# End of a recurrence on one core: where the last tile's squares are summed, and which PSUM banks the two halves use

## Chip, cores and metric

The kernel runs on 1 core of one Trainium2 chip. The metric is the device time of one execution, in microseconds (us). All data is fp32. Engines: PE (matmul; PEld is its weight load), DVE (VectorE), ACT (ScalarE), POOL (GpSimd), SP (issues DMAs).

## What is computed

The reference has two layers. The first is a recurrence over 1024 tokens for each of 4 x 1024 channels, run forward and backward, and a quotient of its two sums, gated by a sigmoid. The second works on its output x in two blocks: normalised logits of 16 slots against all tokens, the best 4 tokens per slot, a gather of those rows, and an attention of all tokens over the slots.

```
def step(carry, x):
    a, b = carry
    ekv_t, ek_t = x
    a = a * decay + ekv_t
    b = b * decay + ek_t
    return ((a, b), (a, b))
...
num = nf + nb - ekv + euk * vf
den = df + db - ek + euk
base = jax.nn.sigmoid(r.astype(jnp.float32)) * (num / jnp.maximum(den, 1e-08))
out = base * (0.8 + 0.2 * tf)
...
for _ in range(NB):
    logits = _rms(x, norm_pre_w) @ compete_w.T + compete_b
    slot_logits = jnp.swapaxes(logits, 1, 2)
    vals, idx = jax.lax.top_k(slot_logits, k_eff)
    ...
```

So a logit is the product of a token's row with a slot's weights, divided by the root of the mean of that row's squares. The change concerns how those two sums, products and squares, are finished at the end of the first layer.

## The kernel before

Channels lie on the 128 partitions and tokens along the free axis: a tile is 128 channels x 1024 tokens, and there are 32 tiles (4 batches b x 8 channel groups k), i = 8 b + k, run by the loop at L587. For each tile DVE runs the scans (L323, numerator's backward scan L411), ACT the exponentials and a guess of 1/denominator by Ln and Exp (L426, L428), POOL multiplications (L302, L308, L405, L441, L442, L465), and DVE a Newton step (L452). PE adds the scans into the numerator `num` in PSUM (L373, by the identity matrix), turns the finished tile for storing (L493) and contracts it. The finished tile overwrites its gate tile (`gate`), its squares overwrite `quo` (ACT, L468).

The order on each engine is the order of the code: `pin` keeps it. Waits are put in by a tracker of reads and writes of tiles.

`contract` (L470 to L483) multiplies a tile by the slots' weights (`lhs[:, k]`, source `gate`) or its squares by a column block of ones (`lhs[:, NK]`, source `quo`). Both give 32 rows of `raw`, at partitions 32 b: rows 0 to 15 hold the logits' sums, 16 to 31 the sums of squares. `raw` is one PSUM tile of two banks, 512 tokens in each. At the end the sums of squares lie on other rows than the logits they belong to, so for each half (h = 1 first, then 0) `spread_squares` (L723) copies `raw` to SBUF on DVE (L724) and multiplies it by the matrix `spread` (L725), which puts a square sum on each of the logits' rows, in the PSUM tile `sq`.

The end of the recurrence is L696 to L781, for the last tile, i = 31. In program order: guess in halves; for each half the numerator's backward scan (L416), POOL's products (L438), the addition on PE; contractions of tile 30 among these; then for each half Newton step, product on DVE (L465) and square on ACT (L468); then contractions of tile 31: gate and squares of half 1, gate of half 0; spread of half 1; squares of half 0. Then `norm_root` (ACT: Ln L738, Exp L740, Square L741) and `norm_logits` (DVE: L746, L748, L753, L757, a Newton step on 1/root, and the bias) for half 1, spread of half 0 between them, and the same for half 0. Last, 16 transposes of tiles 30 and 31 (L773) into four banks, four copies on ACT (L779), two stores of rows from ACT's queue (L510), and `hold_clock` (L112), which multiplies the identity by a constant into a bank that nobody reads, seven times.

What follows is the same code for both blocks (`write_slots`): maximum and index on DVE (L833 to L838), the token numbers put in columns by PE (`token_ps`, L851) and cast (L860), an indirect gather of rows on POOL (L863), which needs the stored rows in memory, `hold_clock` again (L885, five in the first block), and the multiplication of the gathered rows (`pmix`, L892), then `pw` (L910), `pkv` (L960), `pk` (L1030). From there on PE works through 32 groups of 128 tokens in each block.

PSUM's tags at the end: `own` (2 banks), `num` (2), `raw` (2), `ptr` (1), `columns` (1).

Of the kernel before, what the change touches and what calls it, by code (L numbers as in the profile page):

```python
# [10 lines left out]
F32 = mybir.dt.float32  # L11
U32 = mybir.dt.uint32
AF = mybir.ActivationFunctionType
ALU = mybir.AluOpType
# [4 lines left out]
P = 128  # L19
B, L, D = 4, 1024, 1024  # L20
S, K, NB = 16, 4, 2
H = 16
HD = D // H
NK = D // P
# [4 lines left out]
EPS = 1e-6  # L29
# [9 lines left out]
def kernel(  # L39
# [25 lines left out]
    nc = tc.nc  # L65
# [12 lines left out]
    pin = tc.keep_in_program_order  # L78
# [33 lines left out]
    def hold_clock(bank, n):  # L112

        for _ in range(n):
            pin(nc.tensor.matmul(bank, ident, npost_bc[:, :512], start=True, stop=True))
# [5 lines left out]
    rec_ps = rec_stack.enter_context(tc.tile_pool(name="rec_ps", bufs=1, space=PSUM))  # L121
# [77 lines left out]
    lhs = rc.tile([P, NK + 1, 2, S], F32, name="lhs")  # L199
# [37 lines left out]
    half = rc.tile([P, B], F32, name="half")  # L237
# [21 lines left out]
    with rec_stack:  # L259

        columns = rec_ps.tile([P, 512], F32, tag="columns", bufs=1, name="columns")
# [2 lines left out]
        nc.vector.tensor_copy(dec_ps, decay)  # L264


        raw = rec_ps.tile([P, L], F32, name="raw")


        HK = NK // 2  # L270
# [40 lines left out]
        def own_tile(i):  # L311
            return rec_ps.tile([P, L], F32, tag="own", bufs=1, name=f"own_{i}")
# [58 lines left out]
        def add(num_ps, h, src, by=ident):  # L371
            pin(
                nc.tensor.matmul(  # L373
                    num_ps[:, ts(h, 512)], by, src, start=False, stop=True, skip_group_check=True
                )
            )
# [44 lines left out]
        def guess(i, both, parts=(every,)):  # L421

            quo = rec.tile([P, L], F32, tag="quo", bufs=2, name=f"quo_{i}")
            b = i // NK
            for part in parts:
                pin(nc.scalar.activation(quo[:, part], both[:, 0, part], AF.Ln))  # L426
                pin(
                    nc.scalar.activation(  # L428
                        quo[:, part],
                        quo[:, part],  # L430
                        AF.Exp,
                        scale=-1.0,
                        bias=half_log_gain[:, b : b + 1],
                    )
                )
            return quo
# [7 lines left out]
        def newton(i, both, quo, num_ps, part=every, out=None):  # L444

            b = i // NK
            den = both[:, 0, part]
            num = num_ps[:, part]
            if out is None:
                den, num = parted(den, i), by_half(num)  # L450
            pin(
                nc.vector.scalar_tensor_tensor(  # L452
                    den if out is None else out[:, part],
                    den,
                    twice_root[:, b : b + 1],
                    num,
                    ALU.subtract,
                    ALU.mult,
                    reverse0=True,
                )  # L460
            )

        def product(i, factor, engine, part=every):
            xk = gate_of(i)[:, part]
            pin(engine.tensor_tensor(xk, xk, factor[:, part], ALU.mult))  # L465

        def square(i, quo, part=every):
            pin(nc.scalar.activation(quo[:, part], gate_of(i)[:, part], AF.Square))  # L468

        def contract(i, src, w, halves=(0, 1)):  # L470

            b, k = i // NK, i % NK
            rows_b = slice(32 * b, 32 * b + 32)
            for h in halves:
                pin(
                    nc.tensor.matmul(  # L476
                        raw[rows_b, ts(h, 512)],
                        lhs[:, w].rearrange("p h s -> p (h s)"),
                        src[:, ts(h, 512)],
                        start=(k == 0 and w == NK),  # L480
                        stop=(k == NK - 1 and w == (NK if i == N - 1 else k)),
                    )
                )  # L483

# [82 lines left out]
        N = B * NK  # L567
        ek, ekv, both, edge, own, quo, num_ps = {}, {}, {}, {}, {}, {}, {}
        flat, pairs, by = {}, {}, {}
        halves = [ts(0, 512), ts(1, 512)]  # L570
# [125 lines left out]
        i = N - 1  # L696
        halves = [(h, ts(h, 512)) for h in (1, 0)]
        raw_sb = rec.tile([P, L], F32, tag="ov", bufs=1, name="raw_sb")
        sq = rec_ps.tile([P, L], F32, tag="own", bufs=1, name="sq")
        eps_col = rc.tile([P, 1], F32, name="eps_col")  # L700
        nc.gpsimd.memset(eps_col, EPS)
        spread_cols = spread.rearrange("p b h s -> p (b h s)")
        quo[i] = guess(i, both[i], [part for _, part in halves])
        square(i - 1, quo[i - 1])

        def contract_half(j, squares, h):
            contract(j, quo[j] if squares else gate_of(j), NK if squares else j % NK, (h,))

        for n, (h, part) in enumerate(halves):
            numerator_half(i, both[i], edge[i], h)  # L710
            gated(i, both[i], quo[i], part)
            add(num_ps[i], h, both[i][:, 1, part])
            if n == 0:
                contract_half(i - 1, False, h)
        contract_half(i - 1, True, 1)
        for squares in (False, True):
            contract_half(i - 1, squares, 0)
        for h, part in halves:
            newton(i, both[i], quo[i], num_ps[i], part, num_ps[i])
            product(i, num_ps[i], nc.vector, part)  # L720
            square(i, quo[i], part)

        def spread_squares(h, part):  # L723
            pin(nc.vector.tensor_copy(raw_sb[:, part], raw[:, part]))  # L724
            pin(nc.tensor.matmul(sq[:, part], spread_cols, raw_sb[:, part], start=True, stop=True))  # L725

        for squares in (False, True):
            contract_half(i, squares, 1)
        contract_half(i, False, 0)
        spread_squares(*halves[0])  # L730
        contract_half(i, True, 0)
        store_turned(i)
        root = rec.tile([P, L], F32, tag="quo", bufs=2, name="root")
        square_root = rec.tile([P, L], F32, tag="ekv", bufs=2, name="square_root")

        def norm_root(part):
            pin(
                nc.scalar.activation(root[:, part], sq[:, part], AF.Ln, scale=1.0 / D, bias=eps_col)  # L738
            )
            pin(nc.scalar.activation(root[:, part], root[:, part], AF.Exp, scale=-0.5))  # L740
            pin(nc.scalar.activation(square_root[:, part], root[:, part], AF.Square))  # L741

        def norm_logits(part):

            t = square_root[:, part]
            pin(nc.vector.scalar_tensor_tensor(t, sq[:, part], EPS * D, t, ALU.add, ALU.mult))  # L746
            pin(
                nc.vector.scalar_tensor_tensor(  # L748
                    t, t, -3.0 * D, root[:, part], ALU.add, ALU.mult
                )  # L750
            )
            pin(
                nc.vector.scalar_tensor_tensor(  # L753
                    t, t, -0.5 / D, raw[:, part], ALU.mult, ALU.mult
                )
            )
            pin(nc.vector.tensor_scalar_add(logits[:, part], t, cb_col))  # L757

        norm_root(halves[0][1])
        spread_squares(*halves[1])  # L760
        norm_logits(halves[0][1])
        norm_root(halves[1][1])
        norm_logits(halves[1][1])

        banks = [rec_ps.tile([P, NT, P], F32, tag="num", bufs=1, name="turn")]
        banks = [
            rec_ps.tile([P, 4, P], F32, tag=tag, bufs=1, name=f"turn_{tag}")
            for tag in ("ptr", "columns")
        ] + [banks[0][:, :4, :], banks[0][:, 4:, :]]
        for n in range(4):  # L770
            for q in range(4):
                block = gate_of(i - 1 + n // 2)[:, ts(4 * (n % 2) + q, P)]
# [3 lines left out]
        for j, stage in ((i - 1, staged(i - 1)), (i, stage_last)):  # L776
            for h in range(2):
                bank = banks[2 * (j - i + 1) + h]
                pin(nc.scalar.copy(stage[:, 4 * h : 4 * h + 4, :], bank))  # L779
            send(j, stage)  # L780
        hold_clock(rec_ps.tile([P, 512], F32, tag="ptr", bufs=1, name="idle"), 7)  # L781
    rc_stack.close()
    keep = ctx.enter_context(tc.tile_pool(name="keep", bufs=1))

# [21 lines left out]
    def bank(tag, name, bufs=2):  # L806
        return wps.tile([P, 512], F32, tag=tag, bufs=bufs, name=name)
# [4 lines left out]
    def write_slots(blk, begin_loads, early, begin):  # L812
# [5 lines left out]
        first, last = blk == 0, blk == NB - 1  # L818
# [63 lines left out]
            pin(nc.gpsimd.memset(score_bias[:, :, C:], 0.0))  # L882
            pin(nc.gpsimd.memset(bias_rows, 0.0))
        early()
        hold_clock(bank("po", f"idle_rows{blk}"), 5 if first else 1)  # L885

        mix_t = half_row(f"mix_t{blk}")
        pmix = bank("psc", f"pmix{blk}")
        for j in range(2):
            for k in range(NK):  # L890
# [5 lines left out]
                        start=(j == 0 and k == 0),  # L896
                        stop=(j == 1 and k == NK - 1),
# [9 lines left out]
        for k in range(NK):  # L907
            for h in range(2):
# [5 lines left out]
                        start=(k == 0),  # L914
                        stop=(k == NK - 1),
# [6 lines left out]
        for h in range(2):  # L922
            part = slots[:, ts(h, 512)]
# [3 lines left out]
        for h in range(2):  # L927
            pt = turned(f"pslots{blk}_{h}").rearrange("p q c -> p (q c)")[:, : 4 * R]
            part = slice(4 * h, 4 * h + 4)
# [92 lines left out]
        for g in range(2):  # L1022
            for i in range(NK):
# [3 lines left out]
                for q in range(4):  # L1027
# [6 lines left out]
                            start=True,  # L1034
                            stop=True,
# [10 lines left out]
            for q in range(4):  # L1046
# [6 lines left out]
                        start=True,  # L1053
# [387 lines left out]
```

## Time and profile before

| | us |
|---|---|
| runs | 1081.12, 1081.73, 1086.94; median 1081.73 |
| the profiled execution | 1085.4 |
| its span, first to last instruction | 1083.2 |
| PE busy | 991.9 (92%) |
| DVE / ACT / POOL busy | 739.6 / 516.1 / 548.1 |
| share of the chain that ended last | PE 59%, POOL 19%, ACT 9%, issue 7%, DVE 3%, DMA 2% |
| last scan's end in the recurrence, to pmix | 394.11 to 426.16 |

The profile is one execution. Every start below is counted from the span's start. The chain of work that ended last is followed back from the last instruction: each step is released by the one before it, or stands behind it on its engine. "Issue" in it is time in which nothing shown was waited for. A PE row counts passes: an fp32 multiplication is two. In the timeline a bracket at a row's end gives its engine's idle time before it and who ended that. In the rows of 1 us stretches the columns are the stretch, its length, PE's busy time with the number of rows, the granted clock (1.00 is full), the DMA engines' busy share and GB/s.

### The profile page before, as it was taken

What the parts mean: (1) busy time and instruction counts of PE and PEld (TensorE: products, weight loads), DVE (VectorE), ACT (ScalarE), POOL (GpSimd) and SP (SyncE); (2) the same over time, 40 slices, a digit from 0 to 9 for tenths busy, and PEclk for the clock granted to TensorE, in tenths of its full rate; (3) what the DMA queues carried; (4) which work ended last, traced back from release to release, by engine and by line L of the source; (5) the groups of instructions that cost most, each with busy time, mean ns of one, the idle gap of its engine ahead of it and who ended that gap; (6) DMA issues with size and microseconds to landing.
All of it is one profiled execution on the core that took longest, in us unless ns stands there. A gap on an engine that the chain in (4) does not pass through costs nothing.

```text
span 1083.2 us, 12290 instructions
## 1 busy us (share of the span) xinstructions
PE 991.9 (92%) x4232; PEld 551.3 (51%) x4232; DVE 739.6 (68%) x1049; ACT 516.1 (48%) x818; POOL 548.1 (51%) x417
## 2 busy tenths in 40 slices
PE   4588898898889888999999999998999999999996
PEld 1223233232323324575666666664574766767663
DVE  7899999999999974244666666565244555555555
ACT  5586877878687742023333343444023333333332
POOL 4999999999999951000222222222000434444344
PEclk9899999999999999999999999999999999999999
DMA  8585574757645273861676877554750445555554
GB/s 265 170 306 159 163 239 147 243 179 268 197 162 165 78 252 98 346 239 59 221 267 256 297 259 259 188 194 154 287 211 21 185 185 213 195 204 190 196 207 155
DMA packets 121790, 218.81 MB, mean 202 GB/s; under 512 B 10928, under 2 KB 76592, under 8 KB 121728
## 3 DMA queue, kind: packets, MB, share of 16 engines
q1 hardware_dynamic: 87872, 199.15, 51.7%
q10 hardware_dynamic: 33280, 16.78, 5.4%
q0 software_dynamic: 576, 2.10, 0.6%
q8 instruction: 33, 0.54, 0.2%
q14 instruction: 29, 0.24, 0.1%
HBM read 150.90 MB, written 67.11 MB: 201 GB/s over the span
## 4 chain that ended last, share of the span: by engine, by line
PE 59%; POOL 19%; ACT 9%; issue 7%; DVE 3%; DMA 2%; SPq 1%; POOLq 0%; ACTq 0%; DVEq 0%
PE psc L1170 21%; PE po L1227 19%; POOL gate L442 5%; POOL ekv L308 4%; POOL gate L465 3%; PE pk L1030 3%; PE pkv L960 3%; PE ptr L1158 3%; PE pv L1098 3%; POOL ek L302 2%; POOL both L405 2%; POOL both L441 2%; ACT quo L428 2%; PE pw L910 1%; ACT quo L426 1%
## 5 line engine op out<-in xcount | busy, mean ns | idle before, releaser
L1170 PE MATMUL psc<-km,xt 128*128 128x272 f32 (+1 forms) x1024 | 238.4, 386 | 0.0
L1227 PE MATMUL po<-vm,e 128*128 128x512 f32 x512 | 230.4, 593 | 0.9 <-ACT e L1217 0.9
L1170 PEld LDWEIGHTS psc<-km,xt 128*128 128x128 f32 x1024 | 189.5, 190 | 29.1
L1204 POOL TENSOR_TENSOR e<-e,den 128x256 f32<-128x256 f32 x64 | 40.5, 632 | 254.2 <-DVE den L1202 233.1
L1227 PEld LDWEIGHTS po<-vm,e 128*128 128x128 f32 x512 | 94.8, 190 | 95.7 <-issue 84.9
L1268 DVE SCALAR_TENSOR_TENSOR y<-y,inv,npost_bc 128x1024 f32<-128x1024 f32 x62 | 79.7, 1285 | 41.2 <-POOL inv L1263 41.2
L1236 DVE TENSOR_TENSOR y<-po,y 128x512 f32<-128x512 f32 x128 | 85.9, 675 | 30.2 <-PE po L1227 29.9
L1256 ACT ACTIVATE junk<-y 128x1024 f32<-128x1024 f32 x63 | 66.7, 1058 | 69.2 <-DVE y L1268 69.1
L1263 POOL TENSOR_TENSOR inv<-mean,minus_half 128x1 f32<-128x1 f32 x64 | 35.5, 555 | 96.8 <-DVE mean L1261 96.8
L441 POOL TENSOR_TENSOR both<-both,quo 128x1024 f32<-128x1024 f32 (+1 forms) x33 | 77.1, 2335 | 11.6 <-ACT quo L428 10.0
L373 PE MATMUL num<-both,ident 128*128 128x512 f32 x128 | 70.6, 675 | 9.9 <-DVE both L411 6.6
L308 POOL TENSOR_TENSOR ekv<-ek,kf 128x1024 f32<-128x1024 f32 (+1 forms) x33 | 76.2, 2311 | 2.6
L323 DVE TENSOR_TENSOR_SCAN both<-columns,ek 128x1024 f32<-128x1024 f32 (+1 forms) x32 | 72.2, 2255 | 7.8 <-POOL gate L465 6.4
L1217 ACT COPY e<-pet 128x256 f32<-128x256 f32 x64 | 23.8, 371 | 112.5 <-PE pet L1216 112.4
L442 POOL TENSOR_TENSOR gate<-gate,quo 128x1024 f32<-128x1024 f32 (+1 forms) x33 | 76.4, 2315 | 0.0
L323 DVE TENSOR_TENSOR_SCAN both<-columns,edges,both 128x1024 f32<-128x1024 f32 x32 | 74.4, 2325 | 2.2 <-ACT edges L344 2.2
L1365 POOL TENSOR_TENSOR y<-y,xin 128x1024 f32<-128x1024 f32 x31 | 73.1, 2358 | 1.4 <-DVE y L1268 1.4
L465 POOL TENSOR_TENSOR gate<-gate,both 128x1024 f32<-128x1024 f32 x31 | 73.4, 2367 | 0.3
L323 DVE TENSOR_TENSOR_SCAN both<-columns,ekv 128x1024 f32<-128x1024 f32 (+1 forms) x32 | 71.4, 2230 | 0.0
L1161 ACT COPY xt<-ptr 128x512 f32<-128x512 f32 x64 | 36.8, 577 | 68.7 <-PE ptr L1158 68.7
L1261 DVE TENSOR_SCALAR mean<-total 128x1 f32<-128x1 f32 x64 | 9.8, 154 | 85.7 <-ACT junk L1256 45.7
L476 PE MATMUL raw<-quo,lhs 128*32 128x512 f32 x128 | 65.3, 602 | 0.0
(214 smaller groups left out, 1646.3 us busy)
## 6 DMA issues: line engine op xcount, KB each, us to landing
y<-rows SPq DMA_DIRECT2D x64, 512.0 KB, 4.3
kf<-in_ft_dram SPq DMA_DIRECT2D x32, 512.0 KB, 5.1
gate<-in_xt_dram SPq DMA_DIRECT2D x32, 512.0 KB, 7.7
turned_rows<-gate SPq DMA_DIRECT2D x32, 512.0 KB, 3.5
xt<-turned_rows SPq DMA_DIRECT2D x32, 512.0 KB, 5.2
rows<-y SPq DMA_DIRECT2D x32, 512.0 KB, 2.9
xin<-in_x_dram SPq DMA_DIRECT2D x32, 512.0 KB, 4.4
rows<-stage ACTq DMA_DIRECT2D x31, 512.0 KB, 4.2
```

The source lines that it names most:

```text
L308: pin(nc.gpsimd.tensor_tensor(ekv[:, part], ek[:, part], kf[:, part], ALU.mult))
L323: nc.vector.tensor_tensor_scan(dst[:, way], dec, src[:, way], start, ALU.mult, ALU.add)
L373: nc.tensor.matmul(num_ps[:, ts(h, 512)], by, src, start=False, stop=True, skip_group_check=True)
L441: pin(nc.gpsimd.tensor_tensor(den, den, quo[:, part], ALU.mult))
L442: pin(nc.gpsimd.tensor_tensor(xk, xk, quo[:, part], ALU.mult))
L465: pin(engine.tensor_tensor(xk, xk, factor[:, part], ALU.mult))
L1170: nc.tensor.matmul(psc[g][:, :n], xt_g[g][:, k, :], maps["km"][:, g // NT, k, :n], start=(k == 0), stop=(k == NK - 1),)
L1227: nc.tensor.matmul(po, et[:, ts(c, P)], vm[:, c, ts(h, 512)], start=(c == 0), stop=(c == 1),)
L1236: pin(nc.vector.tensor_add(half, po, half))
L1256: pin(nc.scalar.activation(junk, src, AF.Square, accum_out=total))
L1268: pin(nc.vector.scalar_tensor_tensor(y[g], y[g], inv[g], npost_bc, ALU.mult, ALU.mult))
L1365: pin(nc.gpsimd.tensor_add(y[g - 1], y[g - 1], xin[g - 1]))
```

## The change

The two halves of `raw` become two tiles of one bank, and those of `sq` too: one in the tag `ptr`, one in the first bank of `own`. The squares of the last tile are no longer contracted into `raw`: after the spread of a half (which then holds the other tiles' sums only), they are contracted on top of it, into the 32 rows of the last batch in `sq`, by a block of ones of 32 columns. The steps are put in another order: Newton step and product of half 1 before the addition or product of half 0, spread before the last tile's gate contractions, both halves' roots on ACT before both halves' last steps on DVE. The transposes use other banks. `hold_clock` gets a new call of three before the last scans, five instead of seven after the transposes, and six instead of five before the first block's `pmix`.

```diff
-        raw = rec_ps.tile([P, L], F32, name="raw")
+        raw = [rec_ps.tile([P, 512], F32, name=f"raw{h}") for h in range(2)]
...
-                        raw[rows_b, ts(h, 512)],
+                        raw[h][rows_b, :],
...
-                        stop=(k == NK - 1 and w == (NK if i == N - 1 else k)),
+                        stop=(k >= NK - 2 and w == (NK if i == N - 2 else k)),
+                        skip_group_check=True,
...
-        sq = rec_ps.tile([P, L], F32, tag="own", bufs=1, name="sq")
+        sq_tile = rec_ps.tile([P, 4, P], F32, tag="ptr", bufs=1, name="sq0")
+        sq = [sq_tile.rearrange("p q c -> p (q c)"), own_tile(N)]
+        own_half, sq[1] = sq[1][:, 512:], sq[1][:, :512]
...
+        ones = lhs[:, NK, 1, 0:1].to_broadcast([P, 2 * S])
...
-        for n, (h, part) in enumerate(halves):
+        def add_half(h, part):
+            add(num_ps[i], h, both[i][:, 1, part])
...
+        def own_squares(h, part):
+            b = i // NK
+            pin(
+                nc.tensor.matmul(
+                    sq[h][32 * b : 32 * b + 32, :],
+                    ones,
+                    quo[i][:, part],
+                    start=False,
+                    stop=True,
+                    skip_group_check=True,
+                )
+            )
+
+        hold_clock(sq[0], 3)
+        for h, part in halves:
             numerator_half(i, both[i], edge[i], h)
             gated(i, both[i], quo[i], part)
-            add(num_ps[i], h, both[i][:, 1, part])
-            if n == 0:
-                contract_half(i - 1, False, h)
-        contract_half(i - 1, True, 1)
-        for squares in (False, True):
-            contract_half(i - 1, squares, 0)
-        for h, part in halves:
-            newton(i, both[i], quo[i], num_ps[i], part, num_ps[i])
-            product(i, num_ps[i], nc.vector, part)
-            square(i, quo[i], part)
...
-        for squares in (False, True):
-            contract_half(i, squares, 1)
-        contract_half(i, False, 0)
+        add_half(*halves[0])
+        contract_half(i - 1, False, 1)
+        newton(i, both[i], quo[i], num_ps[i], halves[0][1], num_ps[i])
+        add_half(*halves[1])
+        product(i, num_ps[i], nc.vector, halves[0][1])
+        square(i, quo[i], halves[0][1])
+        contract_half(i - 1, False, 0)
+        for h in (1, 0):
+            contract_half(i - 1, True, h)
+        newton(i, both[i], quo[i], num_ps[i], halves[1][1], num_ps[i])
         spread_squares(*halves[0])
-        contract_half(i, True, 0)
+        product(i, num_ps[i], nc.vector, halves[1][1])
+        square(i, quo[i], halves[1][1])
+        own_squares(*halves[0])
+        spread_squares(*halves[1])
+        own_squares(*halves[1])
+        for h in (1, 0):
+            contract_half(i, False, h)
         store_turned(i)
...
-        norm_root(halves[0][1])
-        spread_squares(*halves[1])
-        norm_logits(halves[0][1])
-        norm_root(halves[1][1])
-        norm_logits(halves[1][1])
+        for half in halves:
+            norm_root(*half)
+        for half in halves:
+            norm_logits(*half)
...
-            for tag in ("ptr", "columns")
-        ] + [banks[0][:, :4, :], banks[0][:, 4:, :]]
+            banks[0][:, :4, :],
+            banks[0][:, 4:, :],
+            rec_ps.tile([P, 4, P], F32, tag="columns", bufs=1, name="turn_columns"),
+            own_half.rearrange("p (q c) -> p q c", c=P),
+        ]
...
-        hold_clock(rec_ps.tile([P, 512], F32, tag="ptr", bufs=1, name="idle"), 7)
+        hold_clock(rec_ps.tile([P, 512], F32, tag="ptr", bufs=1, name="idle"), 5)
...
-        hold_clock(bank("po", f"idle_rows{blk}"), 5 if first else 1)
+        hold_clock(bank("po", f"idle_rows{blk}"), 6 if first else 1)
```

More of the change, by code (lines that the diff above doesn't have):

```diff
@@ L707, in contract_half, with spread_squares @@
             contract(j, quo[j] if squares else gate_of(j), NK if squares else j % NK, (h,))
-        for n, (h, part) in enumerate(halves):
+        def add_half(h, part):
+            add(num_ps[i], h, both[i][:, 1, part])
+        def spread_squares(h, part):
+            pin(nc.vector.tensor_copy(raw_sb[:, part], raw[h]))
+            pin(nc.tensor.matmul(sq[h], spread_cols, raw_sb[:, part], start=True, stop=True))
+        def own_squares(h, part):
[10 more added lines that the diff above has]
+            )
@@ L723, in spread_squares @@
-        def spread_squares(h, part):
-            pin(nc.vector.tensor_copy(raw_sb[:, part], raw[:, part]))
-            pin(nc.tensor.matmul(sq[:, part], spread_cols, raw_sb[:, part], start=True, stop=True))
-        for squares in (False, True):
-            contract_half(i, squares, 1)
-        contract_half(i, False, 0)
-        spread_squares(*halves[0])
-        contract_half(i, True, 0)
+        add_half(*halves[0])
+        contract_half(i - 1, False, 1)
+        newton(i, both[i], quo[i], num_ps[i], halves[0][1], num_ps[i])
@@ L734, with norm_root, norm_logits @@
         square_root = rec.tile([P, L], F32, tag="ekv", bufs=2, name="square_root")
[L736 to L739, printed above, removed]
+        def norm_root(h, part):
+            pin(nc.scalar.activation(root[:, part], sq[h], AF.Ln, scale=1.0 / D, bias=eps_col))
             pin(nc.scalar.activation(root[:, part], root[:, part], AF.Exp, scale=-0.5))
             pin(nc.scalar.activation(square_root[:, part], root[:, part], AF.Square))
-        def norm_logits(part):
+        def norm_logits(h, part):
             t = square_root[:, part]
-            pin(nc.vector.scalar_tensor_tensor(t, sq[:, part], EPS * D, t, ALU.add, ALU.mult))
+            pin(nc.vector.scalar_tensor_tensor(t, sq[h], EPS * D, t, ALU.add, ALU.mult))
             pin(
@@ L751, in norm_logits @@
             )
[L752 to L756, printed above, removed]
-            pin(nc.vector.tensor_scalar_add(logits[:, part], t, cb_col))
-        norm_root(halves[0][1])
-        spread_squares(*halves[1])
-        norm_logits(halves[0][1])
-        norm_root(halves[1][1])
-        norm_logits(halves[1][1])
+            pin(nc.vector.scalar_tensor_tensor(t, t, -0.5 / D, raw[h], ALU.mult, ALU.mult))
+            pin(nc.vector.tensor_scalar_add(logits[:, part], t, cb_col))
+        for half in halves:
+            norm_root(*half)
+        for half in halves:
+            norm_logits(*half)
         banks = [rec_ps.tile([P, NT, P], F32, tag="num", bufs=1, name="turn")]
         banks = [
-            rec_ps.tile([P, 4, P], F32, tag=tag, bufs=1, name=f"turn_{tag}")
-            for tag in ("ptr", "columns")
-        ] + [banks[0][:, :4, :], banks[0][:, 4:, :]]
+            banks[0][:, :4, :],
[3 more added lines that the diff above has]
+        ]
         for n in range(4):
```

## The prediction

> **What bounds the stage.** I read the page first: PE is busy 92% of the span, but its share in the chain that ended last is 59%, so an average says nothing about the stage changed, which is the 32 us between the last scan of the recurrence and the first multiplication of the gathered rows (L892). For that I read the chain of waits over 355 to 432 us:
>
> ```profile
> 394.24 2.04 PE num L373 x2
> 396.29 1.56 PE raw L476 x2
> 397.85 1.06 PE num L373 x2
> 398.90 5.28 PE raw L476 x12
> ...
> 404.21 0.70 DVE raw_sb L724
> ...
> 412.41 6.28 PE idle L115 x14
> 418.69 0.10 issue
> 418.79 0.30 PE token_ps L851 x4
> ...
> 426.16 5.26 PE pmix L892 x32
> ```
>
> PE carries 394.24 to 404.18 without a gap: both additions to the numerator (L373) and seven contractions into the logits (L476; x12 is six, two passes each). Only then does DVE copy the first half. Later seven idle multiplications (L115) end at 418.69 and the token multiplication starts 0.10 later, although its input (L838) was ready at 417.71. The timeline of 400 to 415 shows why the halves don't overlap in between:
>
> ```profile
> 407.90 0.30 PEld L725 LDWEIGHTS sq<-raw_sb,spread 128*128 128x128 f32 x2 [1.75 <-ACT root L740]
> ...
> 409.14 0.69 DVE L746 SCALAR_TENSOR_TENSOR square_root<-sq,square_root 128x512 f32<-128x512 f32 x1 [1.36 <-PE sq L725]
> ...
> 409.87 0.69 ACT L738 ACTIVATE root<-sq,eps_col 128x512 f32<-128x512 f32 x1 [1.68 <-DVE square_root L746]
> ```
>
> Each half of sq waits for the other half's readers or writer: DVE's first-half L746 waits for the second half's spread, ACT's second-half L738 for that L746. A PSUM tile is ordered as one thing here. Last, PE in stretches of 1 us; the column after the busy one is the granted clock:
>
> ```profile
> 393.00:394.00 1.00, 0.00 (x0) 1.00 1.05 416
> 394.00:395.00 1.00, 0.76 (x1) 0.51 1.05 398
> ...
> 396.00:397.00 1.00, 1.00 (x2) 0.50 1.06 420
> 397.00:398.00 1.00, 1.00 (x3) 0.78 1.06 332
> ...
> 425.00:426.00 1.00, 0.00 (x0) 1.00 0.93 352
> ...
> 429.00:430.00 1.00, 1.00 (x7) 0.50 0.00 0
> ...
> 434.00:435.00 1.00, 1.00 (x4) 0.51 0.00 0
> ```
>
> After 3.29 us without PE work (390.95 to 394.24) the clock is half until 397.6; after 1.56 us (424.60 to 426.16) and a stretch of narrow pmix it is half from 428.4 to 435.
>
> **The change, on this profile's times.** Up to 394.11 (end of DVE's first half scan) nothing moves: the order of POOL and SP is the same row for row, and raw in two tiles adds no wait in the loop. Then:
>
> Three idle multiplications after 390.95 cost 3 x 0.90 (6.28/7) = 2.7 us, ending 393.65. The scan's end at 394.11 covers them with 0.5 us to spare; they would end at 396.3 at half clock. They should keep the clock, so L373 takes 1.06, as at 397.85, to 395.30.
>
> New order on DVE: the first half's Newton step (0.85 from start to next start) no longer waits for both additions. POOL's L441 ends at 395.38, so it runs 395.45 to 396.3. But num is one tile: the second addition now waits for that step, and PE holds tile 30's contractions queued behind it; product (L465) in turn waits for that addition. Addition 396.35 to 397.4; product to 398.15; ACT's square to 398.8. Three contractions at 0.88 (5.28/6) end at 398.3, 399.15 and 400.05.
>
> The copy of the first half needs only the second of these: DVE 399.2 to 399.9. Product of the other half then sits behind that copy, 399.9 to 400.6 (POOL's L442 ends 399.04, no wait), its square ends 401.25, the second copy 401.35. PE: spread 400.05 to 401.15 (1.12), the new contraction of the last tile's own squares to 402.15, spread of the other half to 403.25, its own squares to 404.25. The new operation has no row; it has the shape of raw<-quo (128x512 into 32 rows), which takes 0.88 in a row of its kind and 0.99 after a spread (406.08). Its weights are one column repeated: below 0.88 is excluded[...], above I allow twice that (the first of the two is on the path: 0.9 late); I take 1.0, the row nearest in place. The two contractions of tile 31's squares into raw go, so PE's work is the same; what is gained is that the gate's contractions follow, to 406.0, in the shadow of ACT.
>
> ACT's Ln, Exp, Square take 2.0 per half (406.18 to 408.19): 402.2 to 404.25, then 404.3 to 406.3 with no wait for DVE. DVE's four steps, 2.67 per half (409.14 to 411.81) and 2.78 from half to half: 404.3 and 407.1, ending 409.75 instead of 414.58. Both halves' roots being written first costs ACT nothing. So the maximum begins 4.8 us earlier. Its chain to L838 takes 3.1 (414.61 to 417.71): ready at 412.9.
>
> Idle multiplications, five: they now wait for DVE's second-half L746 (407.8) and follow the transposes (406.0 plus 2.2 = 408.2), ending 412.7 (queued behind their new wait on PE: only the token multiplication). So the token multiplication waits for its data again, 412.95 instead of 418.79: **5.8 us earlier**, of which 1.0 is the idle work that stood in its way.
>
> What comes next late? The rows' writes from ACT: copies after 406.3, second issue about 409.5 instead of 414.39, landing 3.8 later (SP goes on at 418.19 after the last) = 413.3, against the token's cast at 413.5. Cover 0.2 where it was 1.15; if it is gone, up to 0.5. SP's slot loads hang on the same landing, hence start about 1 us later relative to the gather and share the queues' engines with its start: between 0 and 0.4, I take 0.1. Sum: the gather's data is 5.7 us earlier, at 420.4.
>
> Six idle multiplications before pmix instead of five: 0.9 more, ending 419.5; the gather hides them by 0.9. PE's gap shrinks from 1.56 to 0.7 or 0.9. Here a rule speaks against any gain: the Trainium skill, TensorE: Matmul & The Clock Gate, "HAM oscillation", warns of gaps above about 3.4 us only, so by it 1.56 us needs no filler and the sixth is worth nothing. The row says otherwise: half clock two us after that gap. In the second block, at full clock, pmix takes 3.67 and pw 7.11 (5.26 and 8.64 here): 3.1 us between rule and row. The same page (Part 1) says that the activity window runs freely at 3.4 us, so whether a drop falls there is luck of its position; the trace's two stretches of 3.3 and 6.6 us agree. I take it that this loss is in the profiled run and in one of the three runs, not in the median: 1085.4 against 1081.73 is 3.7 us, about that size.
>
> From 426 on everything is carried: the chain is PE (pw, pkv, pk) without a DMA in it, so an earlier pmix is an earlier end. Other edits (flags, names, which bank a transpose uses): same instructions, hidden behind DVE's chain.
>
> **Sum.** Profiled run: span 1083.2 plus 2.2 around it = 1085.4; minus 5.7 = 1079.7, and 1076.6 if the half clock at pmix goes. Against the median: 1081.73 - 5.7 = **1076.0 us**.
>
> **Rivals.**
> - A, the clock drop at 394 is absent in the runs compared. Without it the nine steps take 1.06 + 0.88 + 1.06 + 5.28 = 8.28 instead of 9.94, so before is already 1.7 shorter: gain 4.0, 1077.7. For it: the free window. Against: 3.29 us of gap nearly fill one. Rows landing late gives a like time (gain 5.2 at worst, 1076.5).
> - B, the half clock at pmix comes in most changed runs: 1081.7 - 5.7 + 3.1 = 1079.1. For it: pmix is narrow work and a gap of 0.7 remains.
> - C, the reverse: it is in the median too, and goes: 1072.9.
> - D, slower: the idle multiplications run at half clock and stand in front of pmix. At half clock one takes 1.8; six take 10.8 from 413.9, ending 424.7, 4.3 after the gather's data, and pmix and pw stay slow: 1081.7 - 5.7 + 4.3 + 3.1 = 1083.4. It decides once PE is at half clock when share_ps ends. Against: five idle multiplications run until 412.7, so PE is hardly idle before.
> - E, it doesn't do what it says: if the new contraction or sq's two tiles were still ordered behind each other, only the idle multiplication's 1.0 and the clock's 1.7 would be left: 1079.0. The built order shows each Ln waiting for PE alone, which speaks against it.
>
> **Chances.** Main case 0.50; A 0.24; B 0.10; C 0.06; D 0.04; E 0.04; other 0.02. A measurement here tells about 0.5% (5.4 us, so 1076.3) from no change. Faster by more: main and C, 0.56. Slower by more: 0.02. Rest 0.42. The range takes main, A, B, C and E: 1072.5 to 1080.
>
> **What would show it.** Right: clock 1.00 at 394; raw_sb's first copy near 399.2; the first Ln near 402.2, the second without a wait for DVE; MAX8 near 409.8; token_ps within 0.1 of the index's end (L838); pmix near 420.4. Wrong: the second addition not waiting for Newton (more gain), gather issued over 1 us after the token's cast (rows late), the clock at half during pw, or idle multiplications ending after the gather's landing.

## The result, and the profile after

| us | before | after |
|---|---|---|
| median of 12 runs each | 1081.01 | 1075.82 |
| lowest, highest | 1079.80, 1086.94 | 1074.46, 1080.66 |
| ratio, 95% interval | | 0.9949, 0.9936 to 0.9961 |
| the profiled execution, its span | 1085.4, 1083.2 | 1077.79, 1076.0 |

The change makes the kernel faster by 0.51%, at the bound of what was called faster; the forecast was 1076.0. By the medians the gain is 5.2 us, where 5.7 were forecast. Executions of one kernel differ by several us, so below a stage is read on a clock of its own: time after the end of DVE's first half scan, 394.11 in the profile before and 393.43 after.

| us after that end | before | forecast | after |
|---|---|---|---|
| first half's copy (raw_sb) starts | 10.10 | 5.09 | 5.13 |
| first Ln starts | 12.07 | 8.09 | 8.02 |
| second Ln starts | 15.76 | 10.19 | 10.05 |
| MAX8 starts | 20.50 | 15.69 | 15.47 |
| token multiplication starts | 24.68 | 18.84 | 18.71 |
| pmix starts | 32.05 | 26.3 | 25.78 |
| pmix ends | 37.30 | 30.0 | 30.96 |
| pw ends | 46.39 | 37.5 | 41.23 |

(The forecast's times are those of the prediction minus 394.11. Its last two rows were added for this table: they are the prediction's case without a clock drop there, pmix at 3.67 and pw at 7.11, with 0.45 between.) The chain of waits of the changed kernel, start, length and step:

```profile
393.48 1.12 PE num L373 x2
394.60 0.98 PE raw L476 x2
395.58 1.11 PE num L373 x2
396.69 2.69 PE raw L476 x6
399.38 1.05 PE own L720 x2
400.44 0.99 PE own L725 x2
...
412.14 0.30 PE token_ps L871 x4
...
415.05 6.87 DMA spare<-rows,token
...
422.06 2.34 PE pmix L912 x16
```

The first addition takes 1.12 where it took 2.04. After the second addition three contractions (x6), not six, come before the spread (now L720), and the new contraction L725 takes 0.99. No idle row stands before the token multiplication. But a transfer is now in the chain: pmix's second half waits for the second gather. The timeline of the changed kernel, where brackets show idle time and its cause:

```profile
398.56 0.69 DVE L719 COPY raw_sb<-raw 128x512 f32<-128x512 f32 x1 [0.22 <-PE raw L476]
...
401.45 0.69 ACT L762 ACTIVATE root<-own,eps_col 128x512 f32<-128x512 f32 x1 [0.88 <-PE own L725]
...
403.48 0.69 ACT L762 ACTIVATE root<-sq,eps_col 128x512 f32<-128x512 f32 x1
403.49 0.69 DVE L769 SCALAR_TENSOR_TENSOR square_root<-own,square_root 128x512 f32<-128x512 f32 x1 [3.04 <-ACT square_root L764]
```

The second Ln has no bracket: ACT goes on without waiting for DVE, and DVE waits for its own half's square alone. PE in stretches of 1 us (the column after PE's busy time is the granted clock):

```profile
394.00:395.00 1.00, 1.00 (x4) 1.00 1.03 381
...
421.00:422.00 1.00, 0.18 (x2) 1.00 0.05 20
...
424.00:425.00 1.00, 0.54 (x4) 0.50 0.00 0
...
429.00:430.00 1.00, 1.00 (x4) 0.50 0.00 0
```

The loss at 394 is gone. The one at pmix and pw is not: half clock from 423.5 to 430.3, and pw takes 9.82.

Between the two profiles lie 7.2 us of span: 0.7 arose ahead of the stage, 5.2 in it up to the end of pw (46.39 against 41.23), and 1.4 behind it. The last is in the main another clock drop: from 42.3 us after the end of pw the clock was half for 3.41 us before, and full in the same place after.

```profile
482.77:486.18 3.41, 3.41 (x20) 0.50 0.00 0
```

```profile
476.93:480.34 3.41, 3.41 (x36) 1.00 0.00 0
```

The profile before is the first of the two. The first multiplication into `po` (the attention's output, L1227 before and L1247 after) starts 60.49 us after the end of pw in it, and 58.85 after. Over all the profiles of this document it starts at 60.5 in the six that have this drop (before, e1, e3, e7, e10, e11) and at 58.8 in the seven that don't, kernels with and without the change in both groups: 1.6 us that can't be put down to the change.

### The profile page after: what moved, and what is told of

Read it like the earlier page. It is cut to its first block, busy times and chain, and to the rows that moved or that the text cites. A ratio compares the mean times of both kernels' runs of the same rounds, so it can differ in the third digit from the quotient of the medians.

```text
span 1076.0 us, 12297 instructions
## 1 busy us (share of the span) xinstructions
PE 993.0 (92%) x4236; PEld 552.0 (51%) x4236; DVE 739.4 (69%) x1049; ACT 516.0 (48%) x818; POOL 548.1 (51%) x417
## 4 chain that ended last, share of the span: by engine, by line
PE 58%; POOL 19%; ACT 9%; issue 7%; DVE 4%; DMA 2%; SPq 1%; POOLq 0%; DVEq 0%; ACTq 0%
PE psc L1190 21%; PE po L1247 19%; POOL gate L442 5%; POOL ekv L308 4%; POOL gate L465 3%; PE ptr L1178 3%; PE pk L1050 3%; PE pkv L980 3%; PE pv L1118 2%; POOL ek L302 2%; POOL both L405 2%; POOL both L441 2%; ACT quo L428 2%; PE pw L930 2%; ACT quo L426 1%
## 5 line engine op out<-in xcount | busy, mean ns | idle before, releaser
L1247 PE MATMUL po<-vm,e 128*128 128x512 f32 x512 | 230.4, 593 | 0.9 <-ACT e L1237 0.9
L1247 PEld LDWEIGHTS po<-vm,e 128*128 128x128 f32 x512 | 94.8, 190 | 95.7 <-issue 84.9
L1288 DVE SCALAR_TENSOR_TENSOR y<-y,inv,npost_bc 128x1024 f32<-128x1024 f32 x62 | 79.6, 1284 | 41.2 <-POOL inv L1283 41.2
L1283 POOL TENSOR_TENSOR invn<-mean_n,minus_half 128x1 f32<-128x1 f32 x32 | 17.6, 548 | 91.3 <-DVE mean_n L1281 91.3
```

The lines of the kernel that those rows point to most:

```text
L1247: nc.tensor.matmul(po, et[:, ts(c, P)], vm[:, c, ts(h, 512)], start=(c == 0), stop=(c == 1),)
L1288: pin(nc.vector.scalar_tensor_tensor(y[g], y[g], inv[g], npost_bc, ALU.mult, ALU.mult))
```

## Experiments

Each ran against the kernel before on the same chip; "stage" is the time from the scan's end to the token multiplication, read in one profile. The experiments fall in three groups, run on different chips: the median of the kernel before was 1081.46 beside e1 to e4, 1081.84 beside e5 to e8 and 1081.50 beside e9 to e11. Across groups the ratios compare better than the medians.

**e1: no idle multiplications before the scans**, in the changed kernel.

```diff
-        hold_clock(sq[0], 3)
```

> The changed kernel without the three idle multiplications before the last scans. Measure: from the end of DVE's first half scan to the start of the token multiplication, 24.68 us before the change and 18.71 after. Theory 1 (the clock is part of the gain): PE stands idle over 3 us there, the clock drops to half for some 3 us where the activity window lies so, the first additions take 2.0 instead of 1.1; 20.2 us, and about 1.5 us over the changed kernel (1077.3). Rival (the idle work does nothing, order and banks do all): 18.7, 1075.8.

Measured: median 1080.99, ratio 0.9981 (0.9967 to 0.9994). The stage takes 20.20, as theory 1 said. Its chain of waits:

```profile
393.59 2.05 PE num L373 x2
395.64 1.50 PE raw L476 x2
397.14 1.06 PE num L373 x2
398.20 2.69 PE raw L476 x6
```

These are the lengths of before: the clock is half from 393.3 to 396.7. So the three idle multiplications are worth 1.5 us where the drop occurs. The median, 3.7 above the expected 1077.3, doesn't follow from the stage: of 22 runs 7 lie between 1075.9 and 1077.8, most others near 1081. In this profile pmix and pw ran at half clock again (5.03 and 8.98), and so did the place some 42 us behind pw (478.6 to 482.0). Its span is 3.3 us longer than that of the changed kernel; 1.3 of that stand at the end of pw, the rest behind it. e9 takes the stage up.

**e2: the idle counts alone**, in the kernel before.

```diff
+        hold_clock(rec_ps.tile([P, 512], F32, tag="ptr", bufs=1, name="idle_scan"), 3)
         for n, (h, part) in enumerate(halves):
...
-        hold_clock(rec_ps.tile([P, 512], F32, tag="ptr", bufs=1, name="idle"), 7)
+        hold_clock(rec_ps.tile([P, 512], F32, tag="ptr", bufs=1, name="idle"), 5)
...
-        hold_clock(bank("po", f"idle_rows{blk}"), 5 if first else 1)
+        hold_clock(bank("po", f"idle_rows{blk}"), 6 if first else 1)
```

> The kernel before with nothing but the three counts of idle multiplications changed (3 new ones before the last scans, 5 for 7, 6 for 5). Theory 1: the clock keeps at the scans (1.7) and the token multiplication waits for its data again (1.0): 22.0 us from scan's end to token multiplication, about 1078.3. Rival that it was the idle counts alone: 18.7 and 1075.8. Rival that they do nothing: 24.7 and 1081.

Measured: 1078.65, ratio 0.9979 (0.9956 to 1.0002), an interval that still holds no change. Stage 22.15: 2.5 of the 6.0 us gained in it. In this profile 1.4 of the 2.5 are left at the end of pw: the gathers took 6.7 and 7.2 where they took 5.8 and 5.5.

**e3: banks alone**, in the kernel before.

```diff
-        raw = rec_ps.tile([P, L], F32, name="raw")
+        raw = [rec_ps.tile([P, 512], F32, name=f"raw{h}") for h in range(2)]
...
-        sq = rec_ps.tile([P, L], F32, tag="own", bufs=1, name="sq")
+        sq_tile = rec_ps.tile([P, 4, P], F32, tag="ptr", bufs=1, name="sq0")
+        sq = [sq_tile.rearrange("p q c -> p (q c)"), own_tile(N)]
+        own_half, sq[1] = sq[1][:, 512:], sq[1][:, :512]
```

> The kernel before with nothing but raw and sq in one tile per half (and the transposes in the banks that this leaves); order, squares and idle counts as before. Theory 1: the first copy no longer waits for the other half's contraction, nor the second Ln for DVE: the maximum begins 1.5 us earlier, but seven idle multiplications, which now wait for DVE's second half, still end after the index: 23.4 us from scan's end to token multiplication, about 1079.7. Rival that the false waits were hidden: 24.7 and 1081. Rival that they were all of it: near 19.8 with 1.1 lost to the idle work.

Measured: 1079.94, ratio 0.9981 (0.9965 to 0.9996). Stage 23.29. The chain shows what stops it there:

```profile
411.88 6.28 PE idle L115 x14
...
418.26 0.30 PE token_ps L855 x4
```

**e4: the last squares into raw**, in the changed kernel.

```diff
+        contract_half(i, True, 1)
         newton(i, both[i], quo[i], num_ps[i], halves[1][1], num_ps[i])
-        spread_squares(*halves[0])
         product(i, num_ps[i], nc.vector, halves[1][1])
         square(i, quo[i], halves[1][1])
-        own_squares(*halves[0])
+        contract_half(i, True, 0)
+        spread_squares(*halves[0])
         spread_squares(*halves[1])
-        own_squares(*halves[1])
```

> The changed kernel, but the last tile's squares contracted into raw as before, ahead of the copy and the spread; banks, the rest of the order and idle counts as changed. Theory 1: the copy of the first half waits for one square and one contraction more, the second half's for both: about 1 us later, 19.7 us from scan's end to token multiplication, 1076.8. Rival that the direct contraction is the core of the gain: 2 us or more. Rival that it is worth nothing: 18.7.

Measured: 1077.32, ratio 0.9962 (0.9945 to 0.9978). Stage 19.52: the contraction straight onto the rows is worth 0.8 us of the stage's 6.0. (The edit also puts the first half's copy and spread behind the other half's product, which the squares in `raw` ask for.)

**e5: seven idle multiplications**, in the changed kernel.

```diff
-        hold_clock(rec_ps.tile([P, 512], F32, tag="ptr", bufs=1, name="idle"), 5)
+        hold_clock(rec_ps.tile([P, 512], F32, tag="ptr", bufs=1, name="idle"), 7)
```

> The changed kernel with seven idle multiplications after the transposes instead of five. Theory: they start near 407.0 and end 6.3 later, 1.1 after the index is ready, and hold the token multiplication back by that: 19.8 us from scan's end to token multiplication instead of 18.71, and the time 1.1 us over the changed kernel. Rival that the token multiplication waits for something else (the rows' stores): 18.7.

Measured: 1074.45 (6 runs), ratio 0.9942 (0.9921 to 0.9964): not slower. The stage went as expected, 19.89; yet pmix ended 30.78 us after the scan's end, against 30.96 in the changed kernel. In these profiles the delay of the token was given back before pmix ended. First the issues of the write bias load (SP) and of the first gather (POOL) in e5, then those of the changed kernel:

```profile
414.88 0.52 SPq L81 DMA_DIRECT2D spare<-in_wb_dram  x1
...
415.01 1.19 POOL L883 DMA_INDIRECT spare<-rows,token  x1 [16.34 <-DVE wgt L891]
```

```profile
413.56 1.19 POOL L883 DMA_INDIRECT spare<-rows,token  x1 [15.16 <-DVE wgt L891]
...
414.61 1.39 SPq L81 DMA_DIRECT2D spare<-in_wb_dram  x1
```

The load hangs on the rows' stores, the gather on the token too. In e5 the load is issued first; in the changed kernel 1.05 us after the first gather, and the second gather then needs 6.87 us to land, against 5.26 in e5. In e5 the clock was also full at pmix, which took 3.75 in all.

**e6: the load after pmix**, in the changed kernel.

```diff
-        wb_bc = spare[2][:R, 0, :]
+        wb_bc = spare[0][:R, 0, :]
...
-        move(wb_bc, wb.partition_broadcast(R))
...
+        move(wb_bc, wb.partition_broadcast(R))
         pin(nc.scalar.copy(mix_t[:, : D // 4], pmix[:, : D // 4]))
```

> The changed kernel with the load of the write bias (256 KB) put into the buffer of the first gathered rows, so that it starts only after pmix has read them, 5 us later; all is computed as before. In the changed kernel the second gather landed 6.9 us after its issue (5.5 before) while that load ran beside it, and pmix stood still for 1.1 us between its halves. Theory: contention with that load; the second gather lands in about 5.5, pmix runs through in 3.7, and the clock is kept through pw (7.1) in most runs: from scan's end to the end of pw 37 us instead of 41.2, median 1 to 3 us under the changed kernel. Rival (the gather's own length): no change, 6.9 and 1075.8.

Measured: 1074.80 (6 runs), ratio 0.9943 (0.9923 to 0.9964): about 1 us lower by the medians, within the changed kernel's interval. Gathers in 5.2, pmix in 3.53 without a stop, pw 7.11, its end at 38.2. What kept it from 37 is in the clock and the chain of this run. The first two rows and the last two are e6's; the third is the changed kernel's:

```profile
415.00:416.00 1.00, 1.00 (x2) 0.50 0.63 102
...
417.00:418.00 1.00, 1.00 (x2) 0.50 1.01 410
```

```profile
415.00:416.00 1.00, 1.00 (x3) 1.00 0.84 164
```

```profile
413.73 7.04 PE idle_rows L115 x12
420.77 3.53 PE pmix L911 x32
```

Six idle multiplications took 7.04 instead of 5.4, and pmix started behind them, 1.6 us later than they would have let it at full clock (the first gather landed near 419.0). This is the prediction's rival D. It doesn't come from e6's edit: up to there both kernels run the same instructions, at the same times after the scan's end to within 0.02 us, with the same gap of 1.9 us with little PE work (411.5 to 413.4 in the changed kernel, 411.8 to 413.7 in e6). The clock fell behind it in e6 and e7, and not in the changed kernel.

**e7: one idle multiplication between pmix's halves**, in the changed kernel.

```diff
         for j in range(2):
+            if first and j:
+                hold_clock(bank("po", f"idle_mix{blk}"), 1)
```

> The changed kernel with one idle multiplication (0.9 us) between the two halves of pmix in the first block, in the gap of 1.1 us. Theory that the gap makes the clock drop: pmix ends at the same time, pw takes 7.1 instead of 9.8 in most runs; median 1 to 2 us under the changed kernel. Rival that the narrow multiplications alone make it drop: pw at half clock as often as in the changed kernel, 1075.8 or, where the gather lands earlier, 0.5 more.

Measured: 1076.45, ratio 0.9952 (0.994 to 0.9965), no gain. In its profile both gathers came late (7.5 to 7.8 us, load issued 1.04 after the first), so pmix's wait lay ahead of it, and there was no gap left in its middle: inconclusive on the gap. pmix and pw did run at full clock there, after a first gap of 1.0.

**e8: e6 with seven idle multiplications before pmix.**

```diff
-        hold_clock(bank("po", f"idle_rows{blk}"), 6 if first else 1)
+        hold_clock(bank("po", f"idle_rows{blk}"), 7 if first else 1)
```

> The changed kernel with the late load of the write bias and seven idle multiplications instead of six in front of pmix. Theory: the gap before pmix closes at a price of up to 0.5 us at its start, and the clock is kept in nearly all runs: from scan's end to the end of pw 37.4 us, the runs closer together than those of the late load alone, median within 0.5 us of it. Rival that the clock doesn't drop there any more anyway: 0.5 us over the late load alone. Rival that the load made no difference: at least 0.5 over the changed kernel.

Measured: 1076.05 (7 runs), ratio 0.9951 (0.9931 to 0.9971); pw ends at 37.32 (37.4 expected).

**e9: e8 without the first three; e10: e8's two edits alone, in the kernel before; e11: e8 with six after the transposes.**

```diff
e9:
-        hold_clock(sq[0], 3)
e10, against before, with e6's edit:
-        hold_clock(bank("po", f"idle_rows{blk}"), 5 if first else 1)
+        hold_clock(bank("po", f"idle_rows{blk}"), 7 if first else 1)
e11:
-        hold_clock(rec_ps.tile([P, 512], F32, tag="ptr", bufs=1, name="idle"), 5)
+        hold_clock(rec_ps.tile([P, 512], F32, tag="ptr", bufs=1, name="idle"), 6)
```

> The kernel of the late bias load with seven idle multiplications before pmix (e8), without the three before the last scans. The luck at pmix is taken out of both. Theory (the first idle work is worth what the half clock costs at the scans, 1.5 us, in the runs that had it): 20.2 us from scan's end to token multiplication against 18.7 in e8, median 1.0 to 1.5 us over e8 (1077.3). The median of the changed kernel without the first idle work (e1) lay 5 us over the changed kernel; rival: the first idle work has a second effect at pmix that this kernel must show too, 3 us or more over e8.

> The kernel before with the late load of the write bias and seven idle multiplications before pmix, as in e8; nothing else of the change. Theory: what is left between it and e8 is the stage up to the token multiplication alone, 6.0 us where the clock drops at the scans and 4.3 where not: median 4.5 to 6 us over e8 (1081), and the clock kept at pmix and pw. Rival (much of the measured gain was the clock at pmix, not the stage): within 3 us of e8.

> e8 with six instead of five idle multiplications after the transposes: PE is busy until the token multiplication, which comes about 0.3 us later. In the profiles of e6 and e7 the clock was half from 414.5 to 418 under the idle multiplications before pmix, which then ended 0.9 us after the gather's data (rival D of the prediction). Theory: this fill keeps the clock there; from scan's end to the end of pw 37.6 us, and the median within 0.5 us of e8 or up to 1 under it. Rival: the drop there comes from the transposes and the 32-row multiplications, and stays.

| | median | ratio to before (interval) | stage | pw ends |
|---|---|---|---|---|
| e8 | 1076.05 | 0.9951 (0.9931 to 0.9971) | 18.71 | 37.32 |
| e9 | 1076.81 | 0.9958 (0.9940 to 0.9976) | 20.16 | 38.8 |
| e10 | 1082.01 | 1.0005 (0.9992 to 1.0018) | 24.76 | 43.4 |
| e11 | 1076.69 | 0.9953 (0.9935 to 0.9971) | 19.04 | 37.65 |

e10 is the cleanest measure of the change. Both it and e8 keep the clock from pmix to the end of pw, as e10's chain shows:

```profile
420.61 6.21 PE idle_rows L115 x14
426.82 3.53 PE pmix L891 x32
...
430.80 7.11 PE pw L910 x32
```

and they differ by 6.05 us in the stage and in the end of pw. Their ratios differ by 0.54%, or 5.8 us; since the two come from different groups and each has its interval, this is known to some 2.6 us. The first idle multiplications are worth 1.5 in a profile with the drop (e9); the 0.8 in the median is within the intervals. In e11 the clock stays at full from the scans to the end of pw, but the token comes 0.3 later, as expected; no kernel here is measurably faster than the changed one.

The pair also says what the half clock at pmix and pw is worth in the medians. e10 ends pw 3.0 us earlier than the profile before (43.4 against 46.4), e8 3.9 earlier than the profile after (37.3 against 41.2), yet neither median is lower: 1.0005 (0.9992 to 1.0018) for e10 against before, 0.9951 for e8 against the changed kernel's 0.9949. So this loss belongs to the two profiled executions; as the usual case of either kernel it lies outside these intervals.

## Why the prediction was right, and which terms were off

**The number.** 1076.0 against 1075.82 is in part luck. The 5.7 us were taken from a median of three runs, 1081.73; twelve gave 1081.01. The gain is 5.2 by the medians, and lies between 4.2 and 6.9 by the interval of the ratio.

**The path to the token multiplication: right.** Forecast 5.8 us, measured 5.97. Every step up to it lies within 0.25 us in the table. The forecast's wait of the second addition for the first Newton step is there: it starts 2.15 us after the scan's end, 2.24 forecast. The new contraction, for which no row existed, took 0.99 where 1.0 was taken from the contraction after a spread.

**Its parts.** The clock at 394 was put at 1.7: e1 measures 1.5 in the changed order. The idle work in the token's way was put at 1.0: e2 shows 2.5 for both together, where 2.7 were forecast. e3's banks alone give 1.4, held back by seven idle multiplications; e4 gives the direct contraction 0.8. These two start from different kernels, so they and e2 need not add up to 6.0; what is left falls to the new order, which was not run by itself.

**SP's loads against the gather: mis-sized.** The step "between 0 and 0.4, I take 0.1" had the cause right (SP's loads start 1 us later relative to the gather) and the size wrong, and it named the slot loads, where the one that matters is the write bias load behind them. The second gather took 6.87 against 5.53 before, 1.3 us more, and pmix stood still for 0.88 between its halves. In the profiles it gave back what the idle work's removal had gained: e5 puts that wait back and ends pmix no later.

**The clock at pmix: the step failed as a profile reading.** The sixth idle multiplication was to keep it. In the profile after it did not: PE's gap before pmix was 0.4, but the late second gather opened another of 0.9 in its middle (421.18 to 422.06). That is rival B's result by a cause that I had not named. The sum held since I had taken nothing for this clock in the medians, and e8 and e10 bear that out. My reason for it, that the 3.7 us between the profiled run and the median were about the size of this loss, was weaker than it looked: the same profile holds the drop at 482.8, worth 1.6, which I had not seen. The rule of the Trainium skill (TensorE: Matmul & The Clock Gate, "HAM oscillation") on gaps above about 3.4 us would still miss this case: the clock fell at pmix, with narrow work around, in the four profiles whose PE gaps before and within pmix add up to 1.2 to 1.7 us (before, after, e1, e2), and stayed full in the nine with 1.0 us (e7) or less.

**The rows' stores: hidden, as taken.** The gather was issued 0.87 us after the token's cast in both profiles (420.21 after 419.34, 413.56 after 412.69). It was close: SP, which goes on when the last rows have landed, did so at 412.63, 0.06 us ahead of the end of the cast, where 0.2 were forecast.

**Rivals.** A (no drop at the scans in the runs compared, gain 4.0): not the usual case. The clock is half behind the scans in all five profiles without the three idle multiplications (before, e1, e3, e9, e10) and in none of the eight with them; the medians alone (4.2 to 6.9) rule it out only just. B is in the profile and not in the median. C (1072.9) is refuted by the median and by e10. The half clock of D occurred in e6 and e7. In e6 it cost 1.6 us instead of 4.3, since it lasted one stretch of 3.4 us and not through pw; in e7 the gathers were later still and hid it. E is refuted by the timeline.

**Open.** Why e1's median lies 5.2 over the changed kernel while its stage is 1.5 longer. With the load late and pmix covered (e9) the same edit costs 0.8 in the median. e1's profile has two drops that e9's lacks, at pmix and pw and some 42 us behind pw; how often each falls into a run without a profile is not on record, nor is what makes them so common in e1.

## What to carry to other kernels

Time a chain of small steps from an event just ahead of the change, not from the span's start: runs that scatter by 5 us gave stage times that repeat within 0.1, though the scan's end itself lies anywhere from 393.1 to 396.7 in these profiles. When a step is moved earlier, list what hangs on only one of its inputs, since everything else keeps its place and now collides: here a 256 KB load that had been issued beside the gather came into its middle. Idle work that holds the clock is a queue entry like any other: it was worth 1.5 us where it filled a gap, and held the next step back by 1.2 (e5, at the token) or 1.6 (e6, at pmix) where it ended after the data.

## What the hardware showed that I had not expected

The time from issue to landing of each gather (two of 128 rows of 4 KB) depends on when the 256 KB load is issued against the first. Issued 0.3 before to 0.1 after it (the kernel before, e3, e4, e5): 4.9 to 5.8 us. Issued 0.9 to 1.04 after it (e1, e2, e7): 6.3 to 7.8; in the changed kernel (1.05) 5.5 and 6.9. Without that load at its side (e6, e8, e9, e10, e11): 4.4 to 5.5. The traced packets show what differs. In every profile the gather's own packets start only 1.9 to 2.2 us after its issue. A load issued beside it moves nearly all its bytes before they flow; one issued 1 us later moves its 256 KB in their midst. From 2.5 us after the first gather's issue to the landing of the second (packets, MB, share of the 16 DMA engines' time; q0 is POOL's queue, q1 SP's), before and then after:

```profile
q0 software_dynamic: 282, 1.02, 67.2%
q1 hardware_dynamic: 8, 0.02, 1.4%
```

```profile
q0 software_dynamic: 264, 0.95, 49.6%
q1 hardware_dynamic: 83, 0.27, 16.3%
```

The granted clock fell to half after a gap of 0.9 us within narrow multiplications (after one of 0.4 before them), and under idle multiplications after 1.9 us with little PE work (e6, 411.8 to 413.7). In all 13 profiles a stretch of half clock lasts a whole number of times 3.41 us, and the changes within one profile lie on one grid of that step: in the profile before the stretches start at 394.02, 428.16, 482.77 and 755.84, which is 10, 16 and 80 steps apart. Where the grid lies differs from run to run. So the same idle time costs one execution something and another nothing, as in e6 and the changed kernel, and a single profile doesn't say which is usual. This is the luck of position that the prediction spoke of.
